# A four-layer graph network on one core: x loaded ahead, the check of the adjacency in fixed places, links stored as bytes

## The chip, the cores and the metric

The kernel runs on one NeuronCore of a Trainium2 chip, as one program. The metric is the device time of one execution in microseconds (us). A core has TensorE (PE, matrix products), VectorE (DVE), ScalarE (ACT), GpSimd (POOL) and SyncE (SP, which here only issues DMAs). SBUF is the on-chip memory of 128 partitions, PSUM the banks that PE writes, and the large arrays lie in HBM.

## The reference

There are 8 graphs with the same 2048 nodes, 64 features each, and one adjacency `adj` of 2048 x 2048 with entries 0 and 1 (float32, dense near the first nodes and thin elsewhere). Four layers follow one another; each adds to x what it makes of a normalised x:

```python
h = jnp.maximum(_layernorm(x, axis=-1), 0.0)
x = x + _L0_gnn_ref(h, H, adj, ...)   # hyperedges: softmax pooling, tanh scores, plus (adj / deg) @ (h @ W_ind)
...
x = x + _L1_gnn_ref(h, adj, ...)      # Chebyshev: h, adj h, 2 adj adj h - h; a weight for each node
...
x = x + _L2_gnn_ref(h, adj, ...)      # three message steps with a two-layer net
...
x = x + _L3_gnn_ref(h, adj, ...)      # attention: softmax of adj * leaky_relu(e_src + e_dst), all pairs
```

## The kernel before, in words

A node tile is 128 nodes (16 tiles, `NT`), a chunk 512 nodes (4 chunks, `NC`). x lies in HBM as four pairs of graphs, 128 rows (two graphs x 64 features) by 2048 nodes, so a chunk of x is 1 MB.

*First stage* (`start`). Two pieces of work have no need of each other. The layernorm of layer 0 goes chunk by chunk: the x chunk is loaded into a ring of two buffers `x_ch`; PE takes off the mean (`center`), ACT squares (`sq`), DVE and ACT in turn clip at zero (`xr`), PE sums the squares (`to_rows`), ACT takes the root and DVE the reciprocal (`std`, L299 and L300). That is the first part of `norm_parts`, up to its `yield`. In the second part PE spreads `std` over the features and DVE multiplies (L641). `features` then makes `h @ W` in two layouts, with ACT copying the results out of PSUM (L676 and L682).

The other piece is `check_adj`. It reads adj tile by tile (16 loads of 1 MB, L390, into four row buffers), ACT squares the tile into bfloat16 and sums it (L391, `squares`, a ring of four), DVE compares the tile with its square and counts (L392, `equal`): an entry equal to its square is 0 or 1. POOL clears the diagonal block (L395) and stores the squares in HBM as `links` (L399), and PE notes which blocks hold a link (`seen`). After the last tile a chain of small steps counts degrees and lists and writes one number, `flag` (L423). All engines read it and branch: with 0 they take the short path, which uses the lists of links. That path runs here.

The order in time is made by a planner that walks the program and hands each engine its instructions, by readiness in its own model of time and by place in the program. So in the profile rows of the check lie between parts of the norms although the program lists all of them after the last norm. `behind` (L193) is how the program overrules it: an instruction so marked is issued after the one that was traced before it on the same engine. On each engine instructions then run in that fixed order, and one that waits holds up all behind it. DMA loads issued by SP wait in SP's own order.

*Neighbour search* (`neighbours`, run in `convolution_near` of layer 1). For 15 tiles of nodes POOL gathers the tile's rows of `links` by an indirect DMA (L2043) into one of two buffers, DVE multiplies them in place with the node numbers (L2052), and takes the highest numbers eight at a time (MAX8, L2058), blotting out those it has (L2062). It is cut in single steps by `yield`; the convolution calls one step per pair of blocks. Around it PE makes the products `pk`, DVE multiplies them with the node's embedding (L1867), and POOL adds them up (L1872).

Of the kernel before, what the change touches and what calls it, by code (L numbers as in the profile page):

```python
# [7 lines left out]
F = mybir.dt.float32  # L8
BF = mybir.dt.bfloat16
# [126 lines left out]
class Kernel:  # L136
# [8 lines left out]
    def __init__(self, tc, ctx, a):  # L145
        self.tc, self.nc, self.a = tc, tc.nc, a
        self.flip = 0
        self.short = False
        self.consts = ctx.enter_context(tc.tile_pool(reuse_waits="tile", name="consts", bufs=1))

        dram = ctx.enter_context(tc.tile_pool(reuse_waits="tile", name="dram", bufs=1, space=bass.MemoryType.DRAM))
        self.xs = [
            [a["xT"][:, :, c * CW : (c + 1) * CW].rearrange("q p n -> p q n") for c in range(NC)]
        ]


        self.h_rows = dram.tile([N, ROW], F, name="h_rows")
        self.g_rows = dram.tile([N, NB * D], F, name="g_rows")
        self.order3 = dram.tile([P, 2, NT], I32, name="order3")

        self.links = dram.tile([N, N], BF, name="links")
        self.sent = [dram.tile([N, NB * D], F, name=f"sent{i}") for i in range(5)]


        self.f_rows = dram.tile([N, WIDE], F, name="f_rows")
        self.att_rows = dram.tile([N, NB * D], F, name="att_rows")
        self.rdeg = dram.tile([NT, P], F, name="rdeg")

        self.h_sums = [dram.tile([8, P, CW], F, name=f"sums{q}") for q in range(NP)]
        self.h_parts = [dram.tile([P, 3, N], BF, name=f"parts{q}") for q in range(NP)]  # L170
        for i in range(3):
            self.xs.append([dram.tile([P, NP, CW], F, name=f"x{i}_{c}") for c in range(NC)])
        self.setup()
# [194 lines left out]
    def check_adj(self, pool, slots, seen, ps, flag):  # L368


        nc, adj = self.nc, self.a["adj"]
        limit = self.limits(pool)
        over = pool.tile([P, limit.shape[1] + 2], F, name="over")
        ones = pool.tile([P, P], BF, name="ones")
        nc.vector.memset(ones, 1.0)
        rows = [slots.tile([P, 2, N], F, name=f"rows{i}", tag=f"q{6 + i}") for i in range(2)]
        squares = slots.tile([P, 4, N], BF, name="squares", tag="q8")
        same = pool.tile([P, NT], F, name="same")
        deg = pool.tile([P, NT], F, name="deg")
        own = pool.tile([P, NT], F, name="own")  # L380
        equal = pool.tile([P, N], BF, name="equal")
        one = pool.tile([P, 1], BF, name="one_bf")
        nc.vector.memset(one, 1.0)
        nc.sync.dma_start(
            own, bass.AP(tensor=adj.tensor, offset=adj.offset, ap=[[N + 1, P], [P * (N + 1), NT]])
        )
        for t in range(NT):
            row, sq = rows[t // 2 % 2][:, t % 2], squares[:, t % 4]
            here = slice(t * P, (t + 1) * P)
            nc.sync.dma_start(row, adj[here])  # L390
            nc.scalar.activation(sq, row, AF.Square, accum_out=deg[:, t : t + 1])  # L391
            nc.vector.scalar_tensor_tensor(  # L392
                equal, row, 1.0, sq, op0=OP.mult, op1=OP.is_equal, accum_out=same[:, t : t + 1],
            )
            nc.gpsimd.affine_select(  # L395
                out=sq[:, here], in_=sq[:, here], compare_op=OP.not_equal, fill=0.0, base=0,
                pattern=[[-1, P]], channel_multiplier=1,
            )
            nc.gpsimd.dma_start(self.links[here], sq)  # L399
            for i in range(FAR):  # L400
                c = (HUBS + i) * P
                self.mm(
                    seen[:, t, i : i + 1], sq[:, c : c + P], one,
                    start=t == 0 and i == 0, stop=t == NT - 1 and i == FAR - 1,
                )
        hm = slots.tile([P, NT, D], F, name="hm", tag="q9")
        nc.sync.dma_start(hm, self.a["H"].rearrange("(t p) e -> p t e", p=P))
        nc.vector.tensor_scalar(hm, hm, 0.0, None, op0=OP.is_gt)
        nc.vector.tensor_reduce(self.deg[:, 0], hm, axis=AX.X, op=OP.add)
        self.count_nodes(pool, ones, limit, over, 0, ps)  # L410
        nc.vector.tensor_sub(self.deg[:, 1], deg, own)
        self.count_nodes(pool, ones, limit, over, 1, ps)
        bad = pool.tile([P, 1], F, name="bad")
        nc.vector.tensor_reduce(bad, same, axis=AX.X, op=OP.add)
        nc.vector.tensor_scalar(over[:, -2:-1], bad, float(N * NT), None, op0=OP.is_lt)
        nc.vector.tensor_scalar(self.edges, seen, 0.0, None, op0=OP.is_gt)
        self.count_lists(pool, ones, limit, over, ps)
        nc.vector.tensor_reduce(bad, over, axis=AX.X, op=OP.max)
        pt = ps.tile([P, CW], F, name="chain")[:1, :P]
        nc.tensor.transpose(pt, bad, self.ident)  # L420
        one = pool.tile([1, 1], F, name="one")
        nc.vector.tensor_reduce(one, pt, axis=AX.X, op=OP.max)
        nc.vector.tensor_scalar(flag, one, 0.0, None, op0=OP.is_gt)  # L423

        nc.vector.memset(self.self_weight, 0.0)
        alone = self.edges.rearrange("p t i -> p (t i)")[:, HUBS * FAR :: FAR + 1]
        weight = self.self_weight[:, HUBS:]
        nc.vector.tensor_scalar(weight, alone, -1.0, 1.0, op0=OP.mult, op1=OP.add)
        nc.vector.tensor_mul(weight, weight, own[:, HUBS:])
        nc.vector.tensor_scalar_max(deg, deg, 1.0)  # L430
        nc.vector.reciprocal(deg, deg)
        pr = ps.tile([P, CW], F, name="chain")[:NT, :P]
        nc.tensor.transpose(pr, deg, self.ident)
        rows = pool.tile([NT, P], F, name="rows")
        nc.vector.tensor_copy(rows, pr)
        nc.sync.dma_start(self.rdeg, rows)
# [192 lines left out]
    def start(self, pool, slots):  # L629
# [6 lines left out]
        with tc.tile_pool(reuse_waits="tile", name="k00", bufs=1) as k:  # L636
            ww = self.block_diag(k, a["W"], "ww")
            hn = Halves(slots, "hn", ("q0", "q1"), False)

            def write(q, ch, xr, scale):  # L640
                nc.vector.tensor_mul(hn(q)[:, ch * CW : (ch + 1) * CW], xr, scale)  # L641

            with (
                tc.tile_pool(reuse_waits="tile", name="links_ps", bufs=1, space=PSUM) as lps,
                tc.tile_pool(reuse_waits="tile", name="ln", bufs=2) as w,
                tc.tile_pool(reuse_waits="tile", name="ln_ps", bufs=6, space=PSUM) as ps,
            ):
                seen = lps.tile([P, NT, FAR], F, name="seen")
                self.h = (
                    hn, Halves(slots, "h_t", ("q2", "q3"), False),  # L650
                    Halves(slots, "h_n", ("q4", "q5"), True),
                )

                def bank():
                    return ps.tile([P, CW], F, name="bank")

                for ch in range(NC):
                    x = self.load_x(w, 0, ch)
                    xr = w.tile([P, NP, CW], F, name="xr", bufs=1)
                    sq = w.tile([P, NP, CW], F, name="sq", bufs=1)  # L660
                    std = w.tile([P, CW], F, name="std", bufs=1)
                    self.norm(ch, x, xr, sq, std, bank, write)
                    if ch > 0:
                        self.features(ww, ch - 1, bank)
                self.check_adj(k, slots, seen, lps, flag)
                self.features(ww, NC - 1, bank)
        return flag

# [1068 lines left out]
    def convolution_near(self, slots, k, ps, conv):  # L1737
# [7 lines left out]
        with tc.tile_pool(reuse_waits="tile", name="conv", bufs=2) as w:  # L1745
# [64 lines left out]
            for place, ch in enumerate(chunks):  # L1810
# [3 lines left out]
                if place == 1:  # L1814
                    words = k.tile([P, 4 * CW], F, name="near_rows", tag="early", bufs=1)
                    near = self.neighbours(
                        steps.k, conv.order, range(1, NT),
                        words.bitcast(BF).rearrange("p (i n) -> p i n", i=2),
                        words.bitcast(I32), w.tile([P, N], F16, name="line", bufs=1),
                    )  # L1820
                ahead = iter(()) if ends else product(place + 1)
# [208 lines left out]
        self.nc.sync.dma_start(self.order3, order)  # L2030
        yield

    def neighbours(self, k, order, tiles, rows, whole, line):

        nc, near = self.nc, self.near
        nc.gpsimd.iota(whole, pattern=[[1, N]], base=1, channel_multiplier=0)
# [11 lines left out]
        fetch(0)  # L2048
        for i, t in enumerate(tiles):
            fetch(i + 1)  # L2050
            row = rows[:, i % 2].bitcast(F16)
            self.behind(nc.vector.tensor_mul(row, rows[:, i % 2], line))  # L2052
            yield
            most = -(-NEAR[t] // 8)
# [1232 lines left out]
```

## Time and profile before

| what | value |
|---|---|
| time, median of 3 runs | 1926.74 us (1921.63 to 1930.95) |
| the profiled execution | 1917.82 us, span 1916.1 us |
| busy share of the span | PE 88%, DVE 72%, POOL 56%, ACT 43% |
| mean granted clock of TensorE | 0.943 |
| moved by DMA | 305.25 MB, 159 GB/s on average |
| first stage, 0 to 97 us, moved by DMA | 30.09 MB in the first 100 us |
| flag written | 95.91 + 0.14 us after the start |

The profile is that of one execution. The page gives busy time by engine, then 40 slices of the span in tenths, then the chain of waits that ended last, the costliest groups of instructions and the DMA issues. Busy time includes waiting inside an instruction. The views by stretch, by group and by wait used below cut the same execution into parts.

### The profile page before, as it was taken

The page shows a single profiled execution, that of the slowest core. Times are in us where ns is not written, and L with a number is a line of the kernel's source. Part 1 is how long each engine was busy: PE and PEld are TensorE (multiplying, and loading weights), DVE is VectorE, ACT ScalarE, POOL GpSimd, SP SyncE. Part 2 cuts the span into 40 slices and gives each one's busy share as a digit, 9 for nine tenths or more (in the row PEclk, how much of TensorE's full clock was granted, in tenths as well). Part 3 has the DMA queues.
Part 4 walks back from the last instruction along what each step waited for, and adds up shares of the span by engine and source line. Part 5 has one row for each costly group of instructions (what it writes and reads, how often), then busy time and mean ns, then how long its engine had stood idle before and what let it go on. Part 6 is the DMA issues. An engine that isn't in the chain of part 4 may idle for free.

```text
span 1916.1 us, 22580 instructions
## 1 busy us (share of the span) xinstructions
PE 1682.1 (88%) x7139; PEld 959.6 (50%) x7139; DVE 1376.8 (72%) x2281; ACT 818.7 (43%) x1650; POOL 1078.3 (56%) x1039
## 2 busy tenths in 40 slices
PE   5888899998997788899999999889999999679885
PEld 2446766664333454344343435358777575345432
DVE  6887778884677878778888777557666676558874
ACT  5732544454666654222111010057676754466300
POOL 1101366776762755887687756547373641677760
PEclk8998999998998899999999989999999999789887
DMA  9741223334545774324142232168788774766655
GB/s 340 286 124 46 67 93 101 112 124 159 172 131 152 212 226 155 97 81 125 39 110 98 72 106 77 51 210 274 242 253 261 234 244 148 241 175 180 183 174 196
DMA packets 127372, 305.25 MB, mean 159 GB/s; under 512 B 29681, under 2 KB 33537, under 8 KB 122113
## 3 DMA queue, kind: packets, MB, share of 16 engines
q0 software_dynamic: 45328, 149.60, 26.7%
q1 hardware_dynamic: 79600, 149.82, 23.5%
q10 hardware_dynamic: 2304, 4.20, 0.6%
q8 instruction: 60, 0.98, 0.2%
q14 instruction: 80, 0.65, 0.1%
HBM read 240.41 MB, written 63.14 MB: 158 GB/s over the span
## 4 chain that ended last, share of the span: by engine, by line
PE 35%; DMA 7%; POOL 5%; DVE 5%; issue 4%; ACT 1%; SPq 0%; DVEq 0%; POOLq 0%; ACTq 0%
PE pk L177 17%; PE acc L177 11%; POOL ring L2976 3%; DMA raw<-sent,index 3%; PE bank L177 1%; PE pn L177 1%; DMA ring<-f_rows,near 1%; POOL raw L2646 1%; PE pw L177 1%; PE pz L1955 1%; PE side L177 1%; DMA q<-att_rows 1%; POOL half L1872 1%; PE first L177 1%; PE p L177 1%
## 5 line engine op out<-in xcount | busy, mean ns | idle before, releaser
L2646 POOL DMA_INDIRECT raw<-sent,index x300 | 314.0, 1047 | 286.1 <-DVE part_lo L2664 143.0
L2663 ACT CAST part_hi<-raw 128x512 fp32r<-128x512 f32 x352 | 211.3, 619 | 299.9 <-PE acc L177 202.1
L2664 DVE TENSOR_TENSOR part_lo<-raw,part_hi 128x512 fp32r<-128x512 f32 x352 | 263.6, 769 | 88.4 <-ACT part_hi L2663 80.5
L177 PE MATMUL pk<-q,w 128*128 128x512 f32 (+1 forms) x768 | 305.6, 613 | 5.4 <-DVE q L1753 3.3
L1872 POOL TENSOR_TENSOR half<-half,y 128x512 f32<-128x512 f32 x210 | 263.9, 1287 | 68.5 <-DVE y L1867 67.8
L177 PE MATMUL acc<-q,ident 128*128 128x512 f32 x416 | 202.8, 613 | 23.4 <-DVE q L3066 17.0
L177 PEld LDWEIGHTS pk<-q,w 128*128 128x128 f32 (+1 forms) x768 | 116.1, 190 | 156.8 <-issue 108.7
L177 PE MATMUL acc<-part_lo,weights 128*128 128x512 f32 x365 | 164.5, 452 | 28.4 <-DVE part_lo L2664 28.1
L177 PE MATMUL acc<-part_hi,weights 128*128 128x512 f32 x365 | 171.4, 471 | 19.9 <-ACT part_hi L2663 19.2
L1867 DVE SCALAR_TENSOR_TENSOR y<-pk,bias,q 128x512 f32<-128x512 f32 x210 | 148.2, 744 | 46.6 <-POOL half L1872 23.3
L2976 POOL DMA_INDIRECT ring<-f_rows,near x121 | 140.0, 1157 | 62.8 <-issue 29.2
L177 PEld LDWEIGHTS acc<-q,ident 128*128 128x128 f32 x416 | 76.8, 194 | 97.2 <-issue 42.8
L2355 POOL TENSOR_TENSOR q<-q,beta 128x512 f32<-128x512 f32 x57 | 76.0, 1335 | 71.4 <-DVE beta L2331 32.6
L177 PEld LDWEIGHTS acc<-part_lo,weights 128*128 128x128 f32 x365 | 71.1, 195 | 86.4 <-DVE part_lo L2664 74.0
L177 PEld LDWEIGHTS acc<-part_hi,weights 128*128 128x128 f32 x365 | 70.8, 194 | 69.7 <-ACT part_hi L2663 37.5
L177 PE MATMUL pp<-adj,x_ind_hi 128*128 128x512 f32 x256 | 90.4, 470 | 0.5 <-DVE q L882 0.3
L3047 DVE TENSOR_TENSOR q<-ring,e 128x1024 f32<-128x1024 f32 x58 | 70.1, 1219 | 9.0 <-PE acc L177 8.8
L2632 ACT CAST hub_weights<-dense 128x384 fp32r<-128x384 uint8 x80 | 40.4, 510 | 83.4 <-PE acc L177 83.2
L300 DVE RECIPROCAL std<-std 128x512 f32<-128x512 f32 (+1 forms) x17 | 53.8, 3162 | 30.5 <-ACT std L299 30.5
L2355 POOL TENSOR_TENSOR q<-q,coef 128x512 f32<-128x512 f32 x57 | 63.0, 1106 | 21.0 <-DVE q L2378 17.6
L177 PE MATMUL pp<-adj,x_ind_lo 128*128 128x512 f32 x256 | 72.6, 403 | 0.0
L2563 POOL DMA_INDIRECT listed_raw<-in_adjT_dram,cell x60 | 62.9, 1048 | 16.5 <-issue 15.6
(504 smaller groups left out, 3431.0 us busy)
## 6 DMA issues: line engine op xcount, KB each, us to landing
rows<-in_adj_dram SPq DMA_DIRECT2D x16, 1024.0 KB, 9.5
adj_t<-in_adjT_dram SPq DMA_DIRECT2D x64, 256.0 KB, 3.1
own<-sent SPq DMA_DIRECT2D x52, 256.0 KB, 4.2
raw<-sent SPq DMA_DIRECT2D x52, 256.0 KB, 3.7
sent<-u SPq DMA_DIRECT2D x48, 256.0 KB, 3.2
q<-x SPq DMA_DIRECT2D x9, 1024.0 KB, 5.0
links<-squares POOLq DMA_DIRECT2D x16, 512.0 KB, 8.6
sent<-q SPq DMA_DIRECT2D x32, 256.0 KB, 2.2
```

Source lines behind the costliest of these rows:

```text
L177: self.nc.tensor.matmul(out, lhsT, rhs, start=start, stop=stop)
L300: nc.vector.reciprocal(std, std)
L1867: nc.vector.scalar_tensor_tensor(y, pks[b, half], bias[:, b : b + 1], emb[:, b], op0=OP.add, op1=OP.mult,)
L1872: nc.gpsimd.tensor_add(acc, acc, y)
L2355: self.nc.gpsimd.tensor_tensor(x, x, by.unsqueeze(2).to_broadcast([P, NB, D]), op=OP.mult)
L2563: self.kern.behind(nc.gpsimd.indirect_dma_start(raw[:, i], None, rows, bass.IndirectOffsetOnAxis(ap=self.cell[:, c + i : c + i + 1], axis= ...
L2632: self.nc.scalar.copy(to, self.lists.dense[:, :, i * P : (i + 1) * P])
L2646: self.nc.gpsimd.indirect_dma_start(raw, None, self.rows[:], bass.IndirectOffsetOnAxis(ap=self.lists.index[:, c : c + 1], axis=0),)
L2663: nc.scalar.copy(hi, raw)
L2664: nc.vector.tensor_sub(lo, raw, hi.bitcast(F))
L2976: self.nc.gpsimd.indirect_dma_start(to, None, self.kern.f_rows[:], bass.IndirectOffsetOnAxis(ap=index, axis=0))
L3047: nc.vector.tensor_tensor(y.rearrange("n i (b f) -> n i b f", b=NB), block[:, i : i + 2, : NB * D].rearrange("n i (b f) -> n i b f", b=NB) ...
```

## The change

Three things are changed. The four x chunks of layer 0 are loaded at the start, straight into the space in which `h_n` (the features by node) will be written later; `std` and `xr` get two buffers. The check becomes a generator that stops after each tile, its squares and comparisons are marked with `behind`, and `start` calls for tiles at fixed places: the first part of the next chunk's norm, two tiles, the second part of this chunk's norm, one tile, the features of the chunk before, two tiles. And `links` is stored as one byte for each entry in place of two; since DMAs move the squares as they are in bfloat16, the store on POOL's queue now converts. In the search the gathered rows are bytes, and the product with the node numbers goes to a float16 buffer of its own.

```diff
-        self.links = dram.tile([N, N], BF, name="links")
+        self.links = dram.tile([N, N], U8, name="links")
...
-            nc.scalar.activation(sq, row, AF.Square, accum_out=deg[:, t : t + 1])
-            nc.vector.scalar_tensor_tensor(
-                equal, row, 1.0, sq, op0=OP.mult, op1=OP.is_equal, accum_out=same[:, t : t + 1],
+            self.behind(nc.scalar.activation(sq, row, AF.Square, accum_out=deg[:, t : t + 1]))
+            self.behind(
+                nc.vector.scalar_tensor_tensor(
+                    equal, row, 1.0, sq, op0=OP.mult, op1=OP.is_equal,
+                    accum_out=same[:, t : t + 1],
+                )
             )
...
+            yield
...
+                h_n = self.h[2].tiles
+                xs = [h_n[c // 2][:, TC * (c % 2) : TC * (c % 2 + 1)] for c in (1, 0, 2, 3)]
                 for ch in range(NC):
-                    x = self.load_x(w, 0, ch)
-                    xr = w.tile([P, NP, CW], F, name="xr", bufs=1)
+                    nc.sync.dma_start(xs[ch], self.xs[0][ch])
+
+                def norm(ch):
+                    xr = w.tile([P, NP, CW], F, name="xr")
                     sq = w.tile([P, NP, CW], F, name="sq", bufs=1)
-                    std = w.tile([P, CW], F, name="std", bufs=1)
-                    self.norm(ch, x, xr, sq, std, bank, write)
+                    std = w.tile([P, CW], F, name="std")
+                    return self.norm_parts(ch, xs[ch], xr, sq, std, bank, write)
+
+                check = self.check_adj(k, slots, seen, lps, flag)
+                norms = [norm(0)]
+
+                def rows(n):
+                    for _ in range(n):
+                        next(check)
+
+                next(norms[0])
+                for ch in range(NC):
+                    if ch + 1 < NC:
+                        norms.append(norm(ch + 1))
+                        next(norms[-1])
+                        rows(2)
+                    for _ in norms[ch]:
+                        pass
+                    rows(1)
                     if ch > 0:
                         self.features(ww, ch - 1, bank)
-                self.check_adj(k, slots, seen, lps, flag)
+                        rows(2)
+                for _ in check:
+                    pass
                 self.features(ww, NC - 1, bank)
...
-                        words.bitcast(BF).rearrange("p (i n) -> p i n", i=2),
+                        words[:, : 2 * CW].bitcast(U8).rearrange("p (i n) -> p i n", i=2),
+                        words[:, 2 * CW :].bitcast(F16),
...
-    def neighbours(self, k, order, tiles, rows, whole, line):
+    def neighbours(self, k, order, tiles, rows, row, whole, line):
...
-            row = rows[:, i % 2].bitcast(F16)
             self.behind(nc.vector.tensor_mul(row, rows[:, i % 2], line))
```

## The prediction

> **What bounds the kernel now.** I first read the 40 slices of the page. The engine on top is PE (88% of the span) except in the first two slices, where no engine is full and the DMAs are. The change touches that first stage (0 to 97 us) and the neighbour search in layer 1 (780 to 1240 us), so I cut both out. The busy-time table of the first stage (columns: stretch, length, then busy us of PE, PEld, DVE, ACT, POOL, granted clock, DMA share, GB/s):
>
> ```profile
> 8.00:24.00 16.00, 9.02 (x42) 3.22 (x42) 6.41 (x5) 9.22 (x13) 1.02 (x2) 0.83 1.00 362
> 24.00:48.00 24.00, 19.81 (x96) 9.34 (x97) 23.17 (x23) 15.38 (x21) 4.18 (x10) 0.83 1.00 390
> 48.00:56.00 8.00, 7.76 (x60) 3.16 (x59) 3.93 (x7) 7.35 (x15) 1.66 (x4) 1.00 1.00 400
> 56.00:72.00 16.00, 13.38 (x80) 7.98 (x77) 16.00 (x14) 13.27 (x19) 2.88 (x6) 0.89 0.95 314
> 72.00:80.00 8.00, 4.55 (x71) 2.13 (x73) 5.87 (x8) 7.21 (x10) 0.83 (x2) 1.00 0.99 413
> 80.00:96.80 16.80, 16.50 (x117) 10.06 (x114) 14.93 (x31) 10.50 (x17) 3.52 (x9) 0.90 0.32 129
> ```
>
> From 24 us on DVE is busy 63.9 of 72.8 us and idle 8.9; DMA is full until 80 us and empty after it, while DVE still works through its rows. So the DMAs run close to DVE, but DVE ends the stage. The list of waits of 0 to 98 us (us in total, times, longest) agrees:
>
> ```profile
> DVE xr L294 <- ACT sq L291: 10.2, 4, 7.1
> ACT squares L391 <- DMA rows<-in_adj_dram: 7.8, 3, 4.9
> DVE equal L392 <- ACT squares L391: 5.2, 3, 3.6
> DVE std L300 <- ACT std L299: 2.8, 3, 1.6
> SPq L390 <- DVE equal L392: 37.0, 10, 6.0
> SPq L264 <- PE bank L177: 6.5, 2, 4.2
> ```
>
> SP's row loads wait 37.0 us for DVE to free a row buffer: DVE sets the pace. The last line is SP standing still for an x buffer, with row loads queued behind it. The costs, by groups of 0 to 97 us, and the end, by the timeline of DVE:
>
> ```profile
> L392 DVE SCALAR_TENSOR_TENSOR equal<-rows,squares 128x2048 bf16<-128x2048 f32 x16 | 36.7, 2294 | 5.2 <-ACT squares L391 5.2
> L391 ACT ACTIVATE squares<-rows 128x2048 bf16<-128x2048 f32 x16 | 30.4, 1904 | 9.2 <-DMA rows<-in_adj_dram 7.8 <-DMA links<-squares 1.3
> L300 DVE RECIPROCAL std<-std 128x512 f32<-128x512 f32 x4 | 13.4, 3350 | 2.8 <-ACT std L299 2.8
> ...
> 88.97 2.42 DVE L392 SCALAR_TENSOR_TENSOR equal<-rows,squares 128x2048 bf16<-128x2048 f32 x1
> 95.91 0.14 DVE L423 TENSOR_SCALAR flag<-one 1x1 int32<-1x1 f32 x1
> ```
>
> The last comparison starts at 88.97, the flag is written at 96.05, and all later code waits for it. In layer 1 PE is the limit: 443.87 of 460 us, DVE 345.26. There (min/median/max ns, then starts):
>
> ```profile
> 780.00:1240.00 460.00, 443.87 (x1410) 188.12 (x1409) 345.26 (x412) 67.99 (x133) 332.23 (x273) 0.98 0.28 83
> L2058 DVE MAX8 top<-near_rows x21: 2281/2285/2287, 895.7 to 1201.9; 128x8 f32<-128x2048 f16 x21
> L2052 DVE TENSOR_TENSOR near_rows<-near_rows,line x15: 1211/1215/4055, 887.2 to 1189.7; 128x2048 f16<-128x2048 bf16 x15
> ```
>
> **x first.** The x loads of chunks 2 and 3 go ahead of all rows on SP. This removes SP's 6.5 us, but 2.1 MB more come before row 0: at 390 GB/s 5.4 us, so row 0's square starts at 21.4 instead of 16.07, its comparison after 23.5. In that time DVE does two chunks' first halves (4 xr of 0.69, 2 reciprocals of 3.35) instead of one. Against before, 5.4 us of work (2 xr, one reciprocal, the last 0.6 of the first) move ahead of 24 us and one comparison (2.4) moves behind: DVE has 63.9 - 3.0 = 60.9 us left at 24. The short waits of 80 to 96.8 (1.9) belong to the chain of small steps that ends the check, and stay. Floor of the stage: 24 + 60.9 + 1.9 = 86.8, 10.0 us early.
>
> **Fixed places.** The pins put each square and comparison behind the norm part traced before it. In front of each pinned square on ACT stand 8 or 9 norm or feature steps of 0.6; behind a square that waits for a late row stand the next chunk's norm steps, and PE, DVE and the feature copies wait for those. The idle stretches before (0.8 + 4.1 + 2.1 = 7.0 of 24 to 80 us) were norm parts caught behind squares; norm parts are now issued a chunk ahead, with a second xr and std buffer, so I take away about half, and charge 1 us for row 0's lateness: 10.0 - 3.5 - 1 = 5.5, taken as 5. Bounds: 10 (no idle) to 0 (as much idle as before, in new places). The last features (ACT copies until 99.06 before) finish nearer to the flag; DVE's wait of 0.9 for PE at 99.6 goes: 1 us. The x tiles now lie in h_n, so the feature copies wait for the last read of x, a chunk earlier: nothing, and if that cover went, 0.6 per copy.
>
> **Links as bytes, writing.** The 16 stores of POOL stay 16, with the same issue (0.55 each), but now convert. No conversion by DMA is in this trace. The plain store:
>
> ```profile
> links<-squares POOLq DMA_DIRECT2D x16, 512.0 KB, 8.6
> q0 software_dynamic: 2304, 8.39, 20.5%
> ```
>
> At 390 GB/s a store is 1.34 us, a row load 2.69. At the plain rate row 15 lands at 21.4 + 15 x 2.69 + 12 x 1.34 = 77.8; square 2.1, comparison 2.4, tail 4.7 give 87, so a flag at 91 has 4 us of cover. Bounds: half the time (bytes written count) gains nothing on a DVE-bound stage; k times the time costs (k - 1) x 16.1 - 4. I take the plain rate, the nearest row: 0.
>
> **Links as bytes, reading.** 15 gathers bring 2 KB instead of 4 KB a row (they landed in 5.2 us, nobody waited). The product goes to a buffer of its own, so POOL's next gather no longer waits for the last MAX8: 4.8 us of POOL waits, on an engine with 128 us to spare, 0. The product L2052 now reads a byte operand. Rows: 1.215 with two 16-bit inputs, 2.29 for the comparison with a 32-bit input; I take 2.29, since the operands are no longer both 16-bit: 15 x 1.08 = 16.1 us more of DVE. Cover: each step of the search lies in its own slot between PE's blocks, and DVE has 115 us idle. MAX8, as long as the new product, made PE's loads wait 2.5 us over 21 times: 0.12 x 15 = 1.8, taken as 2. Below nothing: the freed gather waits, at most -1.
>
> The Trainium skill, "VectorE: DVE Perf Modes", section "What auto-detection actually checks", speaks against this part: two results a cycle need every tensor 16-bit, so the byte input loses the rate; by it the product is 2.29 us, and with the row's 1.215 kept the sum would be 2 us lower. "SBUF — State Buffer", section "Who interferes with whom", adds that a DVE step with two SBUF inputs blocks a POOL step that reads SBUF; the one product of 4.055 us here fits that, and by it the longer product would also hold up the adds at L1872, at no price stated.
>
> **Sum.** -5 - 1 + 0 + 2 = -4 us. The profiled execution took 1917.82 (span 1916.1 and 1.7 around it), so 1913.8; it lies 8.9 below the median, so on the median 1922.7, **1923**.
>
> **Rivals.**
> *Full overlap:* DVE never starves, the floor of 86.8 holds and the product stays covered: -10, **1917**. For: the pins leave DVE a queue of rows. Against: ACT needs 33.5 us of squares, 18 of feature copies and 8.8 of norms in the same 60 us.
> *Slow conversion (slower):* stores convert at 2.5 times the plain time. Then rows arrive 24.1 - 4 = 20 us late and nothing covers it, because the ring of four squares and DMA's full share (1.00) leave no slack: -4 + 20 = +16, **1943**; at twice +8, 1935, at three times 1951. It decides from 2.1 times (+9.6). For: an operation the trace has never shown on queues that are already full; against: the same 128 rows of 4 KB are read.
> *Uncovered product (slower):* the 16.1 us of DVE reach PE in full, since PE is at 96% and can't win anything back, and a product twice as long meets POOL's adds twice where it now does once in 15 (4.055, an excess of 2.8): 16.1 + 2.8 - 6 = +13, **1940**; it decides from 15.6 of the 18.9. Against: MAX8's small waits.
> *No effect in the first stage:* the flag stays at 96 and only +2 is left, **1929**. The order in time before already has rows between the norms, so the pins may change little.
>
> **How the numbers follow.** The forecast 0.47, full overlap 0.14, slow conversion 0.17, uncovered product 0.14, no effect 0.08. A measurement of this kernel tells about 0.5% (9.6 us) from no change. Of the forecast's 0.47, 0.05 lie beyond -9.6; of no effect 0.03 beyond +9.6. Faster 0.14 + 0.05 = 0.19, slower 0.17 + 0.14 + 0.03 = 0.34, within 0.47. The likeliest case alone: 1917 to 1930. The range takes in full overlap with 3 us of spread and the slow conversion at 2.5: 1914 to 1943, about 0.15 left out.
>
> **What would show it.** Right: the flag near 91, DVE idle under 6 us between 24 us and the flag, product rows of 2.29, PE waits for them near 2 us, store packets as long as before. Wrong: store landings far above 8.6 us with ACT squares waiting for links or rows; a PE wait for near_rows above 10 us; a flag at 96 or later with DVE waiting for pinned squares.

## The result, and the profile after

The changed kernel takes 1939.8 us (median of 13 runs, 1934.2 to 1945.5) where the kernel before takes 1919.3 (13 runs, 1911.7 to 1931.0): ratio 1.010, 95% interval 1.0083 to 1.0117, so about 19 us slower. Its profiled execution took 1942.23 us with a span of 1940.4 and a mean granted clock of 0.931 (before 1917.82, 1916.1, 0.943).

Where the profile loses the time is read by matching each instruction with the same one of before and taking the difference of their ends. The changed kernel is 9.9 us late at the flag, 12.2 at 600 us (before's time), 19.6 at 780, 22.1 at 1260, and 24.3 at the end. The first stage lost 10 us in place of winning 5. Table of the first stage by stretches, changed kernel, columns as shown before:

```profile
8.00:24.00 16.00, 14.20 (x40) 4.74 (x40) 7.37 (x6) 10.70 (x16) 0.00 (x0) 1.00 1.00 353
24.00:48.00 24.00, 17.58 (x96) 7.95 (x97) 23.12 (x23) 15.95 (x24) 4.37 (x10) 0.79 0.97 300
48.00:56.00 8.00, 6.81 (x61) 4.71 (x60) 4.19 (x6) 6.64 (x10) 1.16 (x2) 1.00 1.06 343
56.00:72.00 16.00, 16.00 (x50) 4.72 (x51) 11.79 (x11) 9.81 (x14) 2.49 (x6) 0.57 0.73 198
72.00:80.00 8.00, 7.85 (x75) 5.59 (x73) 5.27 (x7) 5.38 (x9) 1.66 (x4) 1.00 1.03 325
80.00:96.80 16.80, 16.56 (x113) 10.26 (x113) 12.96 (x17) 13.32 (x20) 3.03 (x7) 0.90 0.68 164
```

Look at VectorE (third pair) from 48 to 80 us: 21.3 of 32 us busy, where it had 25.8. Look at the clock: 0.57 from 56 to 72 us, with TensorE busy for all of the 16 us. The DMA share now falls to 0.73 in that stretch, since row buffers come free late (SP's row loads wait 49.2 us for VectorE's comparisons in the first 100 us, 37.0 before); and 0.68 of it is still needed from 80 to 96.8 us, where it was 0.32 before. What VectorE and ScalarE waited for, first 108 us of the changed kernel (us in total, times, longest):

```profile
ACT q L709 <- PE bank L177: 9.2, 13, 2.3
ACT q L703 <- PE bank L177: 6.2, 8, 1.4
DVE xr L294 <- ACT sq L291: 9.5, 2, 7.1
DVE std L300 <- ACT std L299: 8.0, 4, 4.2
DVE equal L393 <- ACT squares L391: 3.9, 2, 3.7
DVE edges L420 <- PE seen L177: 3.9, 1, 3.9
DVE total L476 <- PE chain L177: 3.7, 1, 3.7
```

The same two lines in the first 108 us of the kernel before (L676 and L682 of before are L703 and L709 now):

```profile
ACT q L676 <- PE bank L177: 4.2, 8, 1.4
ACT q L682 <- PE bank L177: 3.9, 12, 0.5
```

The comparisons and squares themselves cost what they did (36.4 and 30.4 us). The first two lines are the new thing: ScalarE stands at the feature copies until TensorE delivers, 15.4 us in all where it was 8.1, and the pinned squares stand behind it. The timeline of ScalarE ahead of the last two squares shows it (start, length; in brackets the idle time before):

```profile
85.11 0.59 ACT L703 COPY q<-bank 128x512 f32<-128x512 f32 x1 [0.83 <-PE bank L177]
86.41 0.59 ACT L703 COPY q<-bank 128x512 f32<-128x512 f32 x1 [0.71 <-PE bank L177]
...
89.49 0.58 ACT L709 COPY q<-bank 128x512 f32<-128x512 f32 x1 [0.74 <-PE bank L177]
...
91.76 1.91 ACT L391 ACTIVATE squares<-rows 128x2048 bf16<-128x2048 f32 x1
93.57 0.19 ACT L391 ACTIVATION_READ_ACCUMULATOR squares<-rows 128x1 f32 x1
93.66 1.90 ACT L391 ACTIVATE squares<-rows 128x2048 bf16<-128x2048 f32 x1
```

ScalarE needs 8.0 us (83.72 to 91.76) for eight copies that are 0.58 each, and only then come the last two squares. In the kernel before, the last square stood ahead of the same eight copies:

```profile
81.28 1.91 ACT L391 ACTIVATE squares<-rows 128x2048 bf16<-128x2048 f32 x1 [0.34 <-DMA links<-squares]
...
83.64 0.59 ACT L676 COPY q<-bank 128x512 f32<-128x512 f32 x1 [0.36 <-PE bank L177]
```

VectorE of the changed kernel ends the stage so:

```profile
93.25 0.39 DVE L476 TENSOR_REDUCE total<-chain 128x14 f32<-128x224 f32 x1 [3.71 <-PE chain L177]
...
93.83 2.28 DVE L393 SCALAR_TENSOR_TENSOR equal<-rows,squares 128x2048 bf16<-128x2048 f32 x1
...
96.21 2.29 DVE L393 SCALAR_TENSOR_TENSOR equal<-rows,squares 128x2048 bf16<-128x2048 f32 x1
...
103.06 0.38 DVE L420 TENSOR_SCALAR edges<-seen 128x208 bf16<-128x208 f32 x1 [3.87 <-PE seen L177]
...
105.80 0.14 DVE L427 TENSOR_SCALAR flag<-one 1x1 int32<-1x1 f32 x1
```

The last comparison starts 7.2 us later than before, and the tail behind it is 2.7 longer, because `seen` of the last tile waits on TensorE behind 20 feature matmuls of chunk 3. The trace books VectorE's 3.7 us in front of the last two comparisons on `total`, a small step that waits for TensorE and stands ahead of them; the square they need ended at 93.76, so both waits end within 0.6 us. VectorE's idle time from 24 us to the flag is in larger part booked on TensorE and ScalarE's norm steps (`std` 5.1, `total` 3.7, `edges` 3.9, `q` 2.6) than on the squares themselves (3.9): this profile alone does not show that the pins are the cause. The experiments have to.

The stores and the search, changed kernel (issues with KB each and us to landing; a DMA queue of the first 110 us with packets, MB and share; then the product's and MAX8's rows):

```profile
links<-squares POOLq DMA_DIRECT2D x16, 256.0 KB, 7.0
q0 software_dynamic: 2304, 4.20, 20.5%
L2085 DVE MAX8 top<-near_rows x21: 2278/2284/2289, 915.1 to 1223.8; 128x8 f32<-128x2048 f16 x21
L2079 DVE TENSOR_TENSOR near_rows<-near_rows,line x15: 2278/2283/5118, 905.5 to 1211.4; 128x2048 f16<-128x2048 uint8 x15
```

The kernel before, same queue and the same 110 us:

```profile
q0 software_dynamic: 2304, 8.39, 18.7%
```

The converting packets number 2304 as before, with half the bytes, and kept the queue about a tenth longer (20.5% against 18.7% of 110 us; the 20.5% of before in the prediction is of 100 us). The product takes 2.283 us in place of 1.215. The waits from 880 to 1260 us, first of the kernel before, then of the changed one:

```profile
PEld pk L177 <- DVE y L1867: 27.1, 52, 1.7
POOL near_rows L2043 <- DVE top L2058: 3.9, 6, 0.8
PEld pk L177 <- DVE near_rows L2052: 1.5, 3, 0.8
```

```profile
PEld pk L177 <- DVE y L1895: 37.8, 68, 2.0
POOL near_rows L2071 <- DVE near_rows L2079: 36.9, 12, 6.1
PEld pk L177 <- DVE near_rows L2079: 1.0, 2, 0.8
```

TensorE hardly waits for the long product itself (1.0 us). It waits 10.7 us more for `y`, the products with the embedding (L1867, now L1895), which stand behind the long product on VectorE. GpSimd now stands for 36.9 us at gathers, each waiting for the product that frees its byte buffer.

### The profile page after: what moved, and what is told of

Read it like the earlier page. It is cut to its first block, busy times and chain, and to the rows that moved or that the text cites. A ratio compares the mean times of both kernels' runs of the same rounds, so it can differ in the third digit from the quotient of the medians.

```text
span 1940.4 us, 22562 instructions
## 1 busy us (share of the span) xinstructions
PE 1714.1 (88%) x7139; PEld 976.8 (50%) x7139; DVE 1402.6 (72%) x2281; ACT 818.4 (42%) x1650; POOL 1077.0 (56%) x1039
## 3 DMA queue, kind: packets, MB, share of 16 engines
q10 hardware_dynamic: 2304, 4.20, 0.6%
## 4 chain that ended last, share of the span: by engine, by line
PE 31%; DMA 7%; POOL 6%; DVE 6%; issue 6%; ACT 1%; SPq 0%; DVEq 0%; POOLq 0%; ACTq 0%
PE pk L177 15%; PE acc L177 9%; DMA raw<-sent,index 3%; POOL ring L3003 3%; PE bank L177 1%; POOL raw L2673 1%; POOL half L1900 1%; DMA ring<-f_rows,near 1%; PE pw L177 1%; PE pn L177 1%; DMA q<-att_rows 1%; DVE y L1895 1%; PE first L177 1%; DVE part_lo L2691 1%; PE pz L1983 1%
## 5 line engine op out<-in xcount | busy, mean ns | idle before, releaser
L2691 DVE TENSOR_TENSOR part_lo<-raw,part_hi 128x512 fp32r<-128x512 f32 x352 | 274.9, 799 | 95.9 <-ACT part_hi L2690 86.1
L177 PE MATMUL acc<-q,ident 128*128 128x512 f32 x416 | 202.8, 613 | 24.3 <-DVE q L3093 18.3
L1895 DVE SCALAR_TENSOR_TENSOR y<-pk,bias,q 128x512 f32<-128x512 f32 x210 | 148.1, 743 | 45.1 <-POOL half L1900 26.2
L2590 POOL DMA_INDIRECT listed_raw<-in_adjT_dram,cell x60 | 62.9, 1048 | 16.5 <-issue 15.6
```

Of the source, the lines that this page charges most:

```text
L177: self.nc.tensor.matmul(out, lhsT, rhs, start=start, stop=stop)
L1895: nc.vector.scalar_tensor_tensor(y, pks[b, half], bias[:, b : b + 1], emb[:, b], op0=OP.add, op1=OP.mult,)
L2590: self.kern.behind(nc.gpsimd.indirect_dma_start(raw[:, i], None, rows, bass.IndirectOffsetOnAxis(ap=self.cell[:, c + i : c + i + 1], axis= ...
L2691: nc.vector.tensor_sub(lo, raw, hi.bitcast(F))
```

## The experiments

Theory A: the squares pinned behind feature copies starve VectorE. Theory L: the longer product delays `y`, and so TensorE. Their rivals: C, the converting stores are slow; D, x first is what costs; G, GpSimd's waits at the gathers; B, which puts half of the whole loss on the bytes. In each kernel of the first stage the flag and VectorE's idle time from 24 us to the flag are read from the profile; in the search, the growth of the stretch from 780 to 1260 us (between the same instructions). Since TensorE is nearly full there, the growth is also given with the difference in clock loss taken off; clock loss is (1 - granted clock) x length, 15.4 us in this stretch before.

In the later two sets of four the kernel before takes 1971 to 1973 us, against 1919 to 1921 in the result and the first set; totals are therefore given as ratios to the kernel before in the same set, with intervals.

### Set 1: one part of the change at a time

*e1_bytes*, before with the bytes alone:

```diff
-        self.links = dram.tile([N, N], BF, name="links")
+        self.links = dram.tile([N, N], U8, name="links")
...
-            row = rows[:, i % 2].bitcast(F16)
+            # row: a float16 buffer of its own, rows: bytes
             self.behind(nc.vector.tensor_mul(row, rows[:, i % 2], line))
```

> The kernel before with links as bytes alone (byte store, byte gather, product into its own float16 buffer); the first stage is in its old order. Changed less before was +20 us, of which the two traces put +10 on the first stage, about +3 on the stretch of the convolution and leave some 7 without a place. Theory A (the fixed places of the check cost nearly all): flag within 2 us of 96, store packets at the same 20.5% share, product rows 2.28, total +1 to +4 us. Theory B (the bytes cost the half that the first stage does not explain): total +8 to +12 us, with the excess between 640 and 1250 us. Theory C (the converting store is slow): flag at 100 or later, store landings above 8.6 us, squares waiting for links.

Measured: +0.52% (0.32 to 0.72), +10 us. The flag came at 97.39, stores landed in 8.3 us, the product took 2.285. The kernel was 4.2 us late at 780 us and 11.5 at 1260; at equal clock the stretch grew by 5.6. The converting packets took 20.4% of 110 us, as in the changed kernel. TensorE's waits, from 880 to 1260 us:

```profile
PEld pk L177 <- DVE y L1868: 35.6, 63, 2.1
PEld pk L177 <- DVE near_rows L2052: 1.8, 3, 0.8
```

C falls: the flag is 1.3 us late, in an order of the first stage that is that of before. Theory A in its strong form (the pins cost nearly all) falls too: the total lies in B's range, though the excess stands in the search alone, not from 640 us on.

*e2_stage*, the changed kernel with two-byte links and the old search (the diff of e1_bytes, undone in the changed kernel):

> The changed kernel with links back at two bytes and the old neighbour search: only the first stage is changed (x loaded first, two std and xr buffers, check in fixed places, pinned). Theory A (fixed places): flag at 104 to 107 as in the changed kernel, total +10 to +18 us. Theory B (the bytes cost the other half): flag at 104 to 107, total +8 to +11 us. Theory C (the converting store holds up the rows and the stage): flag near 96 or earlier, total within 3 us of before.

Measured: +0.40% (0.17 to 0.64), +7.7 us; flag at 107.47, VectorE idle 20.6 us. The stretch from 780 to 1260 us grew by 0.2 at equal clock. Flag and total lie just outside both A's and B's ranges. So the first stage alone brings the late flag, and the two parts add up: 0.40 + 0.52 = 0.92, against 1.0 (0.83 to 1.17) for the whole.

*e3_stage_free*, e2_stage without the pins:

```diff
-            self.behind(nc.scalar.activation(sq, row, AF.Square, accum_out=deg[:, t : t + 1]))
+            nc.scalar.activation(sq, row, AF.Square, accum_out=deg[:, t : t + 1])
-            self.behind(
-                nc.vector.scalar_tensor_tensor(
...
+            nc.vector.scalar_tensor_tensor(
...
```

> The stage of e2_stage (x first, parts interleaved in the program, links of two bytes) but squares and comparisons of the check are not pinned, so the planner places them. Theory A (the pins starve VectorE): idle time of VectorE between 24 us and the flag falls from 20 to under 10 us, flag at 88 to 96, total -8 to 0 us against before. Theory D (x first makes the rows late, the pins are innocent): flag at 102 or later as in the changed kernel, total +7 or more.

Measured: flag at 96.05, to the hundredth that of before, idle 10.5 us; total +0.30% (0.11 to 0.50). The flag speaks for A and against D. The idle time is half of e2_stage's but no less than before's 8.4, so the 5 us that the prediction saw are not won even without the pins. The total is higher than A allowed, and the first stage doesn't explain it.

*e4_x_first*, before with x loaded first alone:

```diff
+                h_n = self.h[2].tiles
+                xs = [h_n[c // 2][:, TC * (c % 2) : TC * (c % 2 + 1)] for c in (1, 0, 2, 3)]
                 for ch in range(NC):
-                    x = self.load_x(w, 0, ch)
+                    nc.sync.dma_start(xs[ch], self.xs[0][ch])
+                for ch in range(NC):
+                    x = xs[ch]
```

> The kernel before with only the four x chunks loaded at the start into the space of h_n; one xr and one std buffer, whole norm after whole norm, check last in the program, links of two bytes. Theory A: row 0 is squared 5 us later (21.4 in place of 16), the planner fills the gap with norm parts, flag at 90 to 97, total -5 to +2 us. Theory D (x first is what costs): flag at 102 or later, total +7 us or more.

Measured: +0.02% (-0.21 to 0.24), flag at 97.44 with 8.1 us idle. D falls. Row 0 was squared at 21.1 us, 5.1 later, as worked out; but VectorE had 65.4 us of work left at 24 us (before 63.6): with whole norms in the program it did less in the early gap, not more.

### Set 2: what the bytes cost

*e5_act_cast*, e1_bytes with the conversion on ScalarE, after which the product is float16 by float16:

```diff
-            self.behind(nc.vector.tensor_mul(row, rows[:, i % 2], line))
+            self.behind(nc.scalar.copy(row, rows[:, i % 2]))
+            self.behind(nc.vector.tensor_mul(row, row, line))
```

> The kernel before with links as bytes, where ScalarE first turns the gathered bytes into float16 and VectorE then multiplies two float16 operands in place: the product is about 1.21 us again, the gather still waits only for the conversion. With bytes alone the time was +10 us (0.52%), and the stretch from 780 to 1260 us took 7.7 us more than before at an equal loss of clock. Theory L (the 16 us of longer VectorE products delay its products y, for which TensorE waits): +0 to +4 us in all, stretch within 2 us of before, TensorE's waits for y back near 27 us. Theory G (GpSimd stands still at gathers that now come before the product which frees their buffer, and its adds are late): +7 to +11 us, GpSimd again waits over 25 us at the gathers.

*e6_bytes_pinned*, e1_bytes with the gathers late enough on GpSimd:

```diff
-                nc.gpsimd.indirect_dma_start(
+                self.behind(nc.gpsimd.indirect_dma_start(
                     rows[:, i % 2], None, self.links[:],
                     bass.IndirectOffsetOnAxis(ap=order[:, 1, t : t + 1], axis=0),
-                )
+                ))
```

> Bytes as in e1_bytes, with each gather pinned behind the adds traced before it on GpSimd, so that its buffer is free when it is reached. Theory L: the waits of GpSimd at the gathers fall from 37 to under 10 us, but TensorE's waits for y stay above 33 us and the total stays at +7 to +11 us. Theory G: the total falls to 0 to +4 us.

*e7_twice*, before with two-byte links and a second short instruction:

```diff
             self.behind(nc.vector.tensor_mul(row, rows[:, i % 2], line))
+            self.behind(nc.vector.tensor_max(row, row, row))
```

> The kernel before (two-byte links) with a second instruction of the same kind right behind each of the 15 products (the row's maximum with itself, which changes nothing, pinned): 15 x 1.21 = 18 us more VectorE work in the same places, no change of the gathers or of the DMAs. Theory L: +7 to +12 us, the stretch from 780 to 1260 us +6 to +10. Theory G: 0 to +3 us.

*e8_cast_gather*, before with byte links and nothing else; the gather's target stays bfloat16, so the DMA converts back:

```diff
-        self.links = dram.tile([N, N], BF, name="links")
+        self.links = dram.tile([N, N], U8, name="links")
```

> Links stored as bytes, but the gather brings them in as bfloat16, so that the DMA converts a second time and the product stays at 1.21 us in place; each engine's order of instructions is that of before. Theory L and theory G: 0 within 3 us, half the bytes written and read at no price. Theory C (a converting DMA is slow): gathers land far above the 5.2 us of before, VectorE waits for near_rows, and the total is +5 us or more.

Measured:

| kernel | product and its like on VectorE | total | growth 780 to 1260 | clock loss there | growth at equal clock |
|---|---|---|---|---|---|
| changed kernel | 2.28 | +1.0% (0.83 to 1.17) | 2.5 | 11.9 | 5.9 |
| e1_bytes | 2.29 | +0.52% (0.32 to 0.72) | 7.3 | 17.1 | 5.6 |
| e6_bytes_pinned | 2.28 | +0.94% (0.58 to 1.30) | 7.3 | 15.4 | 7.3 |
| e7_twice | 1.22 + 1.22 | +0.60% (0.32 to 0.87) | 3.8 | 15.4 | 3.8 |
| e5_act_cast | 1.23 | +0.38% (0.07 to 0.69) | -1.3 | 15.4 | -1.3 |
| e8_cast_gather | 1.22 | +0.09% (-0.14 to 0.32) | 2.4 | 18.8 | -1.0 |

The other seven short-product kernels (e2 to e4, e10 to e13) grow by -1.9 to 0.2 at equal clock. (The 7.7 us at an equal loss of clock that the expectation of e5_act_cast gives for the bytes alone is too high: the table has 5.6.) So every kernel with 16 to 18 us more VectorE work in these slots grows by 4 to 7 us, whether bytes are gathered or not, and none of those with the short product does. The waits from 880 to 1260 us agree; e6_bytes_pinned first, then e7_twice, then e8_cast_gather:

```profile
POOL half L1873 <- DVE y L1868: 85.5, 28, 7.5
PEld pk L177 <- DVE y L1868: 34.1, 56, 3.3
DVE near_rows L2052 <- DMA near_rows<-links,order: 7.0, 2, 5.8
```

```profile
PEld pk L177 <- DVE y L1867: 32.0, 55, 1.8
PEld pk L177 <- DVE near_rows L2053: 1.8, 3, 0.8
```

```profile
PEld pk L177 <- DVE y L1867: 27.8, 55, 1.7
```

G falls twice: with GpSimd's 37 us of gather waits gone (e6) the loss stays, and with 20.0 us of them kept but the product short (e5) the stretch is no longer than before. In e6 the gathers now come so late that VectorE waits 7.0 us for two of them, so the pin costs something of its own; its total, 18 us, lies above the 7 to 11 of L. L holds for the stretch, with two more reservations: e7's stretch grew by less than the 6 expected (its total, 12 us, fits), and e5's total is 0.38% up, 7.5 us, which lies in G's range and not in L's, with nothing in the stretch to explain it. C falls for the gathers too: e8's order on every engine is that of before, VectorE waits for no gather, and the total is unchanged (the profile gives no landing time for this gather).

### Set 3: what the fixed places cost

*e10_pin_equal* is e2_stage with the squares' pin taken off and the comparisons' pin kept. (With the squares alone pinned, every engine gets the same order of instructions as with both pinned; that kernel is e2_stage.)

> The stage of e2_stage (two-byte links) with VectorE's comparisons pinned and ScalarE's squares free. So far the flag came at 96.05 us before, at 107.47 in e2_stage and at 96.05 in e3_stage_free. Theory Q (the pinned squares starve VectorE: each stands on ScalarE behind feature copies that wait for TensorE): flag at 94 to 99, VectorE idle 9 to 13 us from 24 us to the flag. Theory E (the pinned comparisons make VectorE wait): flag at 103 to 108, idle 17 to 21. Total, from e3_stage_free's +0.30%: +0.1 to +0.5% under Q, +0.4 to +0.8% under E.

*e11_rows_first* is e2_stage with one swap:

```diff
                     if ch > 0:
-                        self.features(ww, ch - 1, bank)
                         rows(2)
+                        self.features(ww, ch - 1, bank)
```

> The stage of e2_stage, both pins kept, but the two rows that the program puts after the features of a chunk are put ahead of them, so that the last two squares stand ahead of the features of chunk 2. Theory Q: the part of the idle time that comes from squares behind feature copies goes, VectorE idle 12 to 16 us, flag at 98 to 103. A theory in which x first makes the rows late, or in which a fixed place as such costs: flag stays at 105 to 108, idle near 20.

*e12_mended* is e3_stage_free with the byte links of e8_cast_gather; *e13_pins_cast* is e2_stage with them. On every engine their orders are those of e3_stage_free and e2_stage.

> The whole change without its two suspected costs: x first and parts interleaved as in e3_stage_free (no pins), links stored as bytes and brought back as bfloat16 by the gather as in e8_cast_gather. If the two costs are all there is, the sum of e3_stage_free (+0.30%) and e8_cast_gather (+0.09%): 0 to +0.5%, flag at 95 to 98. If x first has a price of its own outside the first stage: over +0.5%.

> The first stage of the changed kernel with its pins, links as bytes, and the gather converting back, so that the product is 1.21 us again. Against the changed kernel (+0.97%) it lacks only the longer product. Theory L puts 8 us (0.42%) on that: +0.4 to +0.7%, flag at 105 to 108, stretch from 780 to 1260 us within 2 us of before at an equal loss of clock. If the first stage carries the whole loss: +0.8 to +1.1%.

Measured, with the clock loss from 8 us to the flag:

| kernel | squares pinned | flag | VectorE idle, 24 us to flag | clock loss | total |
|---|---|---|---|---|---|
| before | no | 96.05 | 8.4 | 10.2 | |
| e5_act_cast, e8_cast_gather (first stage as before) | no | 96.57, 97.08 | 9.3, 9.4 | 15.4, 15.4 | see set 2 |
| e1_bytes, e6_bytes_pinned, e7_twice (first stage as before) | no | 97.39, 98.65, 98.07 | 9.9, 10.7, 10.0 | 11.9 each | see sets 1 and 2 |
| changed kernel | yes | 105.94 | 19.9 | 15.6 | +1.0% |
| e2_stage | yes | 107.47 | 20.6 | 15.6 | +0.40% (0.17 to 0.64) |
| e13_pins_cast | yes | 103.26 | 17.9 | 10.2 | +0.48% (0.15 to 0.80) |
| e11_rows_first | yes, ahead of the features | 99.13 | 12.6 | 8.5 | +0.12% (-0.16 to 0.39) |
| e3_stage_free | no | 96.05 | 10.5 | 8.5 | +0.30% (0.11 to 0.50) |
| e12_mended | no | 101.09 | 16.0 | 15.5 | +0.26% (-0.02 to 0.54) |
| e10_pin_equal | no, comparisons pinned | 92.14 | 6.9 | 7.8 | +0.01% (-0.23 to 0.24) |

The end of the stage in e10_pin_equal and in e11_rows_first, timeline of VectorE:

```profile
87.91 0.38 DVE L420 TENSOR_SCALAR edges<-seen 128x208 bf16<-128x208 f32 x1 [1.12 <-PE seen L177]
...
91.99 0.14 DVE L427 TENSOR_SCALAR flag<-one 1x1 int32<-1x1 f32 x1
```

```profile
89.99 2.29 DVE L393 SCALAR_TENSOR_TENSOR equal<-rows,squares 128x2048 bf16<-128x2048 f32 x1 [2.34 <-ACT squares L391]
...
98.99 0.14 DVE L427 TENSOR_SCALAR flag<-one 1x1 int32<-1x1 f32 x1
```

Three things follow. First, the comparisons' pin is innocent (92.14, the earliest flag of all, with less idle time than theory Q expected), and it is the squares that must not stand behind feature copies: putting two rows ahead of them wins 4.1 us against e13_pins_cast, at a clock loss of 8.5 and 10.2. In e11_rows_first `total` ends its wait at 93.80, as late as in the changed kernel, but both comparisons are done by then.

Second, in the new orders the flag moves with the granted clock: e12 is 5.0 us behind e3 with 7.0 us more clock loss, e2 4.2 behind e13 with 5.3 more (the two of a pair differ in the links' bytes as well, which moved the flag by 1.3 us in e1_bytes). So the flags expected for e12 (95 to 98) and e13 (105 to 108) were missed, one late, one early. In the order of before it does not: six profiles of it flag from 96.05 to 98.65, and the two with most clock loss, 15.4, at 96.57 and 97.08.

Third, between kernels alike in clock the pins cost 6 to 7 us at the flag (e2 against e12: 6.4; e13 against e3: 7.2). Against the order of before at like clock the pinned order is 7.2 us late (e13, 10.2) to 9 (the changed kernel at 15.6, e5 and e8 at 15.4). So of the 9.9 us that the one profile showed, nearly all belong to the change: 6 to 7 to the pins, and 2 to 3, where the clock loss is 15 us, to a new order that a slower clock delays and the old one not. The totals are too blunt for this: with pins +0.40 and +0.48%, without +0.30 and +0.26%, intervals overlapping; only e10_pin_equal, at +0.01%, stands apart. The pins' price is shown at the flag, from one profile of each kernel, and not in the total.

The stretches from 24 to 48 and from 48 to 80 us, e2_stage and then e13_pins_cast, show the same order at two clocks:

```profile
24.00:48.00 24.00, 16.20 (x87) 6.53 (x88) 23.84 (x23) 16.81 (x23) 4.37 (x10) 0.81 0.92 330
48.00:80.00 32.00, 30.81 (x184) 16.04 (x183) 20.06 (x20) 20.40 (x31) 5.32 (x12) 0.77 0.81 306
```

```profile
24.00:48.00 24.00, 18.03 (x97) 7.62 (x95) 23.12 (x23) 16.02 (x22) 4.37 (x10) 0.79 1.01 305
48.00:80.00 32.00, 28.16 (x189) 15.26 (x187) 21.73 (x23) 22.39 (x31) 5.31 (x12) 0.89 0.96 291
```

e13_pins_cast has all of the change but the long product, and stands at +0.48% where the whole stands at +1.0%: another 10 us for the product's length, as e1_bytes had it. No kernel here is faster than the kernel before.

## Why the prediction was wrong, point by point

Forecast 1923, measured 1939.8: the sign was wrong, and that the time lies inside the range is luck. The range reached that high for a slow conversion that did not come. And the forecast, 4 us of gain, was set on a median of three runs (1926.74) that 13 runs put at 1919.3; the change missed by 24 us, not by 17.

- **x first, the floor.** The work was sized well: 60.9 us of VectorE left at 24 us were forecast, 62.1 were left in the changed kernel and 61.6 in e3_stage_free. The step that turns this floor into time failed.
- **Fixed places: this step failed.** "I take away about half" of the idle stretches: idle time was forecast to fall and it rose, from 8.4 to 19.9 us. The text names what stands in front of each pinned square (8 or 9 steps of 0.6) and charges nothing for it, because it counts their busy time and not their waits for TensorE. Eight copies took 8.0 us. Before, the last square stood ahead of those copies (81.28 and 83.64), and in e10_pin_equal, where squares are free, they alternate with copies. The reading of the idle time was wrong too: of the 7.0 us from 24 to 80 us before, 3.3 were norm parts, 1.6 comparisons waiting for squares, and 2.1 `total` waiting for TensorE, so there was less for norms issued earlier to win. The forecast's flag "near 91" was met by the one kernel in which the comparisons are pinned and the squares free: 92.14.
- **Features tail, -1.** Right behind the flag, wrong in what it left out. The step that waited 0.9 us for TensorE (L518, now L522) comes 2.5 us after the flag in place of 3.5, without a wait. But the same feature matmuls now stand in front of the last `seen`, +2.7 us ahead of the flag: the trace of before had that wait at 0.34 us, and the fixed order moved 20 matmuls into it.
- **Links as bytes, writing, 0.** Right. 2304 packets in both, landing in 7.0 us where it was 8.6, and keeping the queue a tenth longer (20.5 against 18.7% of 110 us); e8_cast_gather, 0.09%. The slow conversion, the rival that stretched the range upwards to 2.5 times the plain time, doesn't exist here: it is 1.1 times.
- **Links as bytes, reading, +2.** The length was right (2.283 against 2.29 forecast, 16 us in all), and so was the direct wait of TensorE (under 2 us forecast; 1.0 in the changed kernel, 1.8 in e1_bytes, 1.5 before). The 2.5 us from which it was worked out belong to all that writes `near_rows`; MAX8's own share was 0.8, once. The term was sized by that direct wait, and this second step failed: TensorE's list of waits names the last instruction, `y`, and not the one that delayed it. The stretch at equal clock puts the term at 4 to 7 us, 5.9 in the changed kernel, so about a third of the added work comes through; the medians of e1 and e7 (10 and 12 us, each uncertain by 4 to 5) put it no lower. The freed gathers brought nothing back: the planner moved them forward, and GpSimd waits there instead.
- **The rivals.** "Uncovered product" has the right mechanism and, by chance, the measured time (1940); its price, all of 16.1 and 2.8 for the adds, was about three times the 5.9 measured, and its stage was to win 6 where it lost 7 to 10. No rival priced the loss that the pins made, though the bound "as much idle as before, in new places" was called the worst end. It was not: nothing in the trace kept idle time from growing. A flag "at 96 or later with DVE waiting for pinned squares" was named as a sign of being wrong; the flag was that late, though most of VectorE's waits carry other names.
- **The sum as measured:** first stage 7 to 10 (pins 6 to 7 of it), product about 6, together 13 to 16; the medians of the parts alone (7.7 and 10) say 18, the whole 19. The difference lies within their intervals. What is left open: e3_stage_free (0.30% up) loses time that its flag doesn't show (e12_mended's 0.26%, 5.1 us, is what its flag is late), while e10_pin_equal and e4_x_first lose none; and 7 us of the changed kernel's profile come between 640 and 780 us in an unchanged order. There the kernel before had 8.5 us of clock loss in its profile, and each of the other 13 had 13.7 to 18.8: that profile was a lucky one in this stretch.

That the product loses its faster form is also what the Trainium skill says in "VectorE: DVE Perf Modes", section "What auto-detection actually checks": two results a cycle need every tensor 16-bit. The 2.283 us in place of 1.215 agree. "SBUF — State Buffer", section "Who interferes with whom", would have the longer product hold up GpSimd's adds; their mean is 1.280 us before and 1.272 after from 880 to 1260 us, so no such price shows on the adds. It is the product that stood: the one product that runs into a row of three adds took 2.84 us longer than its fellows (4.055 before, 5.118 after), and 2.292 in e6_bytes_pinned, where no add lies beside it.

## What to carry to other kernels

An instruction pinned behind others costs their waits and not only their busy time: before fixing an order, add up what the engine in front of the pin waits for, and keep work that feeds the limiting engine ahead of copies that wait for a third. An operation that gets longer on an in-order engine is paid by whoever waits for the instructions queued behind it, so price it by the consumers of those, and not by the wait that the trace puts against its own name. Bytes can be saved where the DMA converts on both sides (e8_cast_gather), so that the compute engine keeps its fast operand types; no time was won by it here. And compare two profiles at like clock loss before a difference of a few us is put down to a change.

## What the runs showed of the hardware

The granted clock stood at half from 57.7 to 71.3 us of the changed kernel, one spell of 13.7 us, while TensorE ran without a gap in the records; e2_stage has the same spell at 59.3 to 72.9. In that time it did matmuls that use 32 rows or 32 columns (2.07 us for two of them in the timeline, where two of the same at 78.73 us, with the clock at 1.0, took 1.12), from 67.1 us on full ones:

```profile
58.94 2.07 PE L177 MATMUL bank<-std,from_rows 32*128 32x512 f32 x2
60.94 1.92 PE L177 MATMUL bank<-sq,to_rows 128*32 128x512 f32 x4
62.79 2.08 PE L177 MATMUL bank<-std,from_rows 32*128 32x512 f32 x4
```

The spells of half clock in the first stage last 3.4, 6.8, 10.2, 13.7 or 17.1 us, multiples of 3.4. The Trainium skill, "TensorE: Matmul & The Clock Gate", section "What's actually happening", has the clock set by windows of that length, which agrees, and the full rate granted after one busy window. The spell bears that out only if the narrow matmuls don't count as busy: its first three windows held narrow ones, and the full rate came after the one window of full ones alone (67.9 to 71.3; in e2_stage 69.5 to 72.9, full ones from 68.6). That was not tried by a run of its own.

DMAs that convert bfloat16 to bytes and back cost no time that the totals can tell (e8_cast_gather +0.09%, -0.14 to 0.32), though the converting store's packets took about a tenth longer. And the same program can take 2.7% longer at another time (1919 to 1921 us in the result and the first set, 1971 to 1973 in the later two): e8_cast_gather, in the order of before throughout, is 12 us behind the profile of before at 1260 us, 41 at 1600 and 58 at the end; the stretch from 1260 to 1600 us is the one in which the DMAs are busiest (247 GB/s before, 226 there). What makes it is open.
